# Edge layer of a four-layer image network: where the sum of VectorE's subtrahends is taken off

## The chip, the cores and the metric

The kernel runs on one core of one Trainium2 chip. The metric is the device time of one execution in microseconds (us); of several executions the median is given. Everything is in 32-bit floating point.

## The reference

The network takes four images of 56 x 56 positions with 128 channels and applies four layers: a windowed attention with a feed-forward part, an edge layer on the rows of the image, a spectral attention and a convolution over rows. The change touches the second layer alone. Its reference is, with one row of 56 nodes for each l:

```python
W1, W2 = (We[:, :f], We[:, f:])
proj_i = jnp.einsum('blnf,of->blno', x, W1)
proj_j = jnp.einsum('blnf,of->blno', x, W2)
edge = jax.nn.relu(proj_i[:, :, :, None, :] + proj_j[:, :, None, :, :] + be)
edge_sum = edge.sum(axis=3)
node_in = jnp.concatenate([x, edge_sum], axis=-1)
node = jax.nn.relu(jnp.einsum('blnc,oc->blno', node_in, Wn) + bn)
```

For each node n of a row, and each of the 56 nodes m of the same row, a ReLU of the sum of two projections is formed, and the 56 results are added. With a the first projection and c the negated second one (bias included), what is added over m is relu(a[n] - c[m]). A group normalisation stands ahead of the layer, and the layer's input is added to its output.

## The kernel before

The four images are taken one after the other, and `edge_layer` runs once for each. It keeps the 128 channels on the partitions, and goes through the image in seven blocks j of 8 rows, 448 nodes (`NB`). In each block it goes through 14 **turns** g, numbered 0 to 13. A turn makes one tile t of four values of m: 4 x 448 = 1792 elements on each partition. The string that follows says which engine makes it:

```python
EDGE_TURNS = "ddpddpdpddpddp"
```

- In the nine turns marked d, VectorE takes the maximum of a and c in one instruction (tile e_td, L967, four buffers). As max(a, c) = relu(a - c) + c, each such value is too large by c[m]. The sum of c over the 36 values of m that VectorE handles is called `rest`, one number for each row and channel (e_rest, L984, a reduce on VectorE, in turn 9).
- In the five turns marked p (2, 5, 7, 10 and 13), GpSimd forms a - c (tile e_tp, L969, three buffers), and ScalarE applies the ReLU in place (L971).

After each turn PE adds the tile to the accumulator e_acc (L974): 16 quadrants of 32 x 32 with an identity as weights, in 32 instructions, since each fp32 product is two. The 128 partitions of the tile are so spread that e_acc has four parts. When all 14 turns are added, ScalarE copies the accumulator to SBUF (e_sums, L986). There is one accumulator, so turn 0 of the next block waits for this copy.

The output of a block (`output`) is made in the next block, after its turn 2: PE multiplies the normalised input by Wn's first half (L940), `rest` by the negated second half (e_nWn, L941), and the four parts of e_sums by the second half (L944), all added into the bank e_po. Each product is again two instructions. In turn 7 of that next block, VectorE finishes the block (`finish`, L949): bias, ReLU, and the sum with the layer's input. After turn 5 of a block ScalarE evacuates the projections of the block that follows (`evacuate`, L932 to L935), and after the copy of the sums PE makes the projections of the block after that (`project`, L922 and L924).

PE, ScalarE and VectorE take the layer's instructions in the order in which the source writes them. GpSimd's order within the layer is chosen by a scheduler. Each engine works through its own queue in order, and a tile's buffer is free for its next use when PE has added it.

Of the kernel before, what the change touches and what calls it, by code (L numbers as in the profile page):

```python
# [13 lines left out]
ALU = mybir.AluOpType  # L14
AX = mybir.AxisListType
# [5 lines left out]
HH = 56  # L21
TOK = HH * HH
NB = 448
# [8 lines left out]
def bc(ap, axis, n):  # L32

    ap = ap.unsqueeze(axis)
    shape = list(ap.shape)
    shape[axis] = n
    return ap.to_broadcast(shape)


def blk(j):  # L40
    return slice(j * NB, (j + 1) * NB)
# [149 lines left out]
def apply_norm(k, out, xt, mr):  # L191
    k.nc.vector.tensor_scalar(out, xt, mr[:, 0:1], mr[:, 1:2], ALU.subtract, ALU.mult)
# [698 lines left out]
EDGE_TURNS = "ddpddpdpddpddp"  # L891


def edge_layer(k, w, x1, st):

    nc, tc = k.nc, k.tc  # L900
    xf = x1.rearrange("p l n -> p (l n)")
    nd = 4 * EDGE_TURNS.count("d")
    quarters = [slice(32 * q, 32 * q + 32) for q in range(4)]
    with ExitStack() as es:
        big = es.enter_context(tc.tile_pool(name="e_big", bufs=1))
        wk = es.enter_context(tc.tile_pool(name="e_wk", bufs=2))
        psum = es.enter_context(tc.tile_pool(name="e_ps", bufs=2, space=PSUM))

        def bank():
            return psum.tile([P, 512], F32, tag="mm", name="e_mm")  # L910

        mr = group_norm_factors(k, wk, bank, st)
        xg = big.tile([P, TOK], F32, name="e_xg")
        for j in range(NBLK):
            apply_norm(k, xg[:, blk(j)], xf[:, blk(j)], mr)
        ready = {}

        def project(j):
            if j >= NBLK:
                return  # L920
            pa = psum.tile([P, 512], F32, tag="pa", name="e_pa")
            nc.tensor.matmul(pa[:, :NB], w.W1, xg[:, blk(j)], start=True, stop=True)  # L922
            pc = psum.tile([P, 512], F32, tag="mm", name="e_pc")
            nc.tensor.matmul(pc[:, :NB], w.W2, xg[:, blk(j)], start=True, stop=True)  # L924
            ready[j] = pa, pc

        def evacuate(j):
            if j >= NBLK:
                return
            pa, pc = ready[j]  # L930
            c = wk.tile([P, 8, HH], F32, name="e_c")
            nc.scalar.activation(c.rearrange("p l m -> p (l m)"), pc[:, :NB], AF.Identity, bias=w.nbe, scale=-1.0)  # L932
            a = wk.tile([P, NB], F32, name="e_a")
            nc.scalar.copy(a, pa[:, :NB])  # L934
            nc.scalar.activation(xf[:, blk(j)], xf[:, blk(j)], AF.Identity, bias=w.bn)  # L935
            ready[j] = pa, a, c

        def output(j, rest, sums):
            po = psum.tile([P, 512], F32, tag="mm", name="e_po")
            nc.tensor.matmul(po[:, :NB], w.Wn[:, 0, :], xg[:, blk(j)], start=True, stop=False)  # L940
            nc.tensor.matmul(po[:, :NB].rearrange("p (l n) -> p l n", l=8), w.nWn, bc(rest, 2, HH),  # L941
                             start=False, stop=False)
            for r in range(4):
                nc.tensor.matmul(po[:, :NB], w.Wnq[:, r, :], sums[:, r, :], start=False, stop=(r == 3))  # L944
            return po

        def finish(j, po):

            nc.vector.scalar_tensor_tensor(xf[:, blk(j)], po[:, :NB], w.nbn, xf[:, blk(j)], ALU.max, ALU.add)  # L949

        with tc.manual_schedule(engines={mybir.EngineType.PE, mybir.EngineType.Activation, mybir.EngineType.DVE}):
            for j in range(2):
                project(j)
                evacuate(j)
            last = None
            for j in range(NBLK):
                pa, a, c = ready.pop(j)
                acc = psum.tile([P, 4, 512], F32, name="e_acc", bufs=1)
                rest = wk.tile([P, 8], F32, name="e_rest")
                at = {"d": 0, "p": nd}  # L960
                for g, e in enumerate(EDGE_TURNS):
                    t = wk.tile([P, 4, 8, HH], F32, tag="e_" + e, name="e_t" + e, bufs=4 if e == "d" else 3)
                    cm = bc(c[:, :, at[e]:at[e] + 4].rearrange("p l m -> p m l"), 3, HH)
                    at[e] += 4
                    if e == "d":
                        am = bc(pa[:, :NB].rearrange("p (l n) -> p l n", l=8), 1, 4)
                        nc.vector.tensor_tensor(t, am, cm, ALU.max)  # L967
                    else:
                        nc.gpsimd.tensor_sub(t, bc(a.rearrange("p (l n) -> p l n", l=8), 1, 4), cm)  # L969
                        tf = t.rearrange("p m l n -> p (m l n)")  # L970
                        nc.scalar.activation(tf, tf, AF.Relu)  # L971
                    for q in range(4):
                        for r, o in enumerate(quarters):
                            nc.tensor.matmul(acc[quarters[q], r, :NB], k.ident[o, o],  # L974
                                             t[o, q].rearrange("p l n -> p (l n)"),
                                             start=(g == 0), stop=(g == len(EDGE_TURNS) - 1))
                    if g == 2 and last:
                        po = output(*last)
                    if g == 5 and last:
                        evacuate(j + 1)  # L980
                    if g == 7 and last:
                        finish(last[0], po)
                    if g == 9:
                        nc.vector.tensor_reduce(rest, c[:, :, 0:nd], AX.X, ALU.add)  # L984
                sums = wk.tile([P, 4, NB], F32, name="e_sums")
                nc.scalar.copy(sums, acc[:, :, :NB])  # L986
                last = j, rest, sums
                project(j + 2)
            finish(last[0], output(*last))


def edge_weights(k, w, pool):

    for n, t in (("nbe", w.be), ("nbn", w.bn), ("nWn", w.Wn[:, 1, :])):
        r = pool.tile(list(t.shape), F32, name="e_" + n)
        k.nc.vector.tensor_scalar_mul(r, t, -1.0)
        setattr(w, n, r)
# [1325 lines left out]
def group_norm_factors(k, pool, bank, st):  # L2323

    nc = k.nc
    mv = pool.tile([P, 2], F32, tag="mv", name="gf_mv")
    nc.vector.bn_aggr(mv, st.rearrange("p a b -> p (a b)"))
    ps = bank()
    nc.tensor.matmul(ps[:, 0:1], k.g4, mv[:, 0:1], start=True, stop=True)
    mr = pool.tile([P, 2], F32, tag="mr", name="gf_mr")  # L2330
    nc.vector.tensor_copy(mr[:, 0:1], ps[:, 0:1])
    t = pool.tile([P, 1], F32, tag="gt", name="gf_t")
    nc.vector.tensor_sub(t, mv[:, 0:1], mr[:, 0:1])
    nc.vector.tensor_mul(t, t, t)
    nc.vector.tensor_add(t, t, mv[:, 1:2])
    ps = bank()
    nc.tensor.matmul(ps[:, 0:1], k.g4, t, start=True, stop=True)
    nc.scalar.activation(t, ps[:, 0:1], AF.Sqrt, bias=k.eps)
    nc.vector.reciprocal(mr[:, 1:2], t)
    return mr  # L2340
# [6 lines left out]
def build(k, packs, I, out):  # L2347
# [3 lines left out]
    with ExitStack() as es:  # L2351
# [12 lines left out]
        with tc.tile_pool(name="w01", bufs=1) as wp, tc.tile_pool(name="io", bufs=1) as io:  # L2364
# [30 lines left out]
            def first_layers(attention, x, to, loaded=False):  # L2395
                if not loaded:
                    nc.sync.dma_start(xw, x)
                xf = io.tile([P, TOK], F32, name="xf")
                attention(k, w0, xw, xf)
                st = io.tile([P, 9, 6], F32, name="x1_st")  # L2400
                mlp(k, w0, xf, xw, x1, st)
                edge_layer(k, w1, x1, st)
                nc.sync.dma_start(to, x1)
# [62 lines left out]
```

## Time and profile before

| what | value |
|---|---|
| median of 8 executions | 3926.8 us (3921.81 to 3933.76) |
| profiled execution, its own time | 3933.63 us |
| its span | 3931.8 us |
| mean granted PE clock, whole span | 0.954 |
| PE, VectorE, ScalarE, GpSimd busy, share of the span | 90%, 73%, 52%, 31% |
| one tile of VectorE (L967), GpSimd (L969), its ReLU (L971) | 2.017, 3.262, 1.697 us |
| reduce (L984), copy of the sums (L986), finish (L949) | 0.444, 1.652, 0.684 us |

The table is to be read with two things in mind. The shares of busy time are averages over all four layers; what holds the edge layer is seen only in its own stretches, of which the first goes from about 610 to 769 us. And the duration of an instruction is longer than the step to the next one on the same engine: seven tiles of VectorE in a row take 13.61 us, 1.94 each. In a line of the timeline, the brackets give how long the engine was idle ahead of the instruction, and whose work ended that idling; "issue" means that the profile shows nothing that it waited for. PEld is the loading of weights for a matmul, and its start shows when PE comes to a turn.

### The profile page before, as it was taken

The page shows a single profiled execution, that of the slowest core. Times are in us where ns is not written, and L with a number is a line of the kernel's source. Part 1 is how long each engine was busy: PE and PEld are TensorE (multiplying, and loading weights), DVE is VectorE, ACT ScalarE, POOL GpSimd, SP SyncE. Part 2 cuts the span into 40 slices and gives each one's busy share as a digit, 9 for nine tenths or more (in the row PEclk, how much of TensorE's full clock was granted, in tenths as well). Part 3 has the DMA queues.
Part 4 walks back from the last instruction along what each step waited for, and adds up shares of the span by engine and source line. Part 5 has one row for each costly group of instructions (what it writes and reads, how often), then busy time and mean ns, then how long its engine had stood idle before and what let it go on. Part 6 is the DMA issues. An engine that isn't in the chain of part 4 may idle for free. (4 is left out here: it accounts for less than half of the span.)

```text
span 3931.8 us, 79380 instructions
## 1 busy us (share of the span) xinstructions
PE 3551.7 (90%) x35416; PEld 1589.2 (40%) x35416; DVE 2883.9 (73%) x2667; ACT 2048.2 (52%) x2056; POOL 1200.9 (31%) x671
## 2 busy tenths in 40 slices
PE   6899988989998898999889999998977989999988
PEld 4322234552222455322245532223446433336554
DVE  6588877748887785888768668885875767775664
ACT  4577755457775454777645567773532002215332
POOL 0000006600000570000037200001860869984665
PEclk8999989999999999999999999998988999999988
DMA  2000000000000000000000000000022047842101
GB/s 94 1 1 1 1 1 19 19 1 1 1 1 1 18 3 17 1 1 1 1 17 3 18 1 1 1 1 0 3 77 94 2 91 164 175 96 83 58 9 50
DMA packets 73497, 111.12 MB, mean 28 GB/s; under 512 B 62141, under 2 KB 63933, under 8 KB 67901
## 3 DMA queue, kind: packets, MB, share of 16 engines
q1 hardware_dynamic: 14460, 93.13, 8.0%
q10 hardware_dynamic: 58688, 12.85, 2.0%
q8 instruction: 279, 4.57, 0.5%
q14 instruction: 70, 0.57, 0.0%
HBM read 79.46 MB, written 26.51 MB: 27 GB/s over the span
## 5 line engine op out<-in xcount | busy, mean ns | idle before, releaser
L641 ACT ACTIVATE f_ring<-f_s 128x1792 f32<-128x1792 f32 (+3 forms) x796 | 1097.8, 1429 | 316.6 <-PE f_s L639 314.4
L594 DVE TENSOR_TENSOR f_acc<-f_acc,f_ring 128x1792 f32<-128x1792 f32 x560 | 1134.0, 2025 | 80.8 <-ACT f_ring L641 27.3
L639 PE MATMUL f_s<-f_qT,f_kT 32*128 32x448 f32 x5376 | 741.0, 573 | 57.6 <-ACT f_ring L641 24.0
L883 POOL TENSOR_TENSOR x<-xf,xw 128x343 f32<-128x343 f32 (+2 forms) x36 | 29.9, 832 | 2134.5 <-issue 2062.2
L600 PE MATMUL f_po<-f_ring,f_va 128*32 128x448 f32 x5376 | 591.2, 547 | 0.0
L967 DVE TENSOR_TENSOR e_td<-e_pa,e_c 128x1792 f32<-128x1792 f32 x252 | 491.4, 2017 | 8.0 <-ACT e_a L934 8.0
L969 POOL TENSOR_TENSOR e_tp<-e_a,e_c 128x1792 f32<-128x1792 f32 x140 | 451.7, 3262 | 143.5 <-PE e_acc L974 104.6
L639 PEld LDWEIGHTS f_s<-f_qT,f_kT 32*128 32x128 f32 x5376 | 269.0, 184 | 538.2 <-ACT f_ring L641 368.2
L974 PE MATMUL e_acc<-e_td,t_shared 32*32 32x448 f32 x8064 | 322.1, 545 | 25.9 <-DVE e_td L967 15.4
L971 ACT ACTIVATE e_tp<-e_tp 128x1792 f32<-128x1792 f32 x140 | 235.2, 1697 | 187.2 <-POOL e_tp L969 187.2
L1568 DVE TENSOR_TENSOR u_ud<-u_px,u_d 112x1792 f32<-112x1792 f32 x144 | 240.2, 1708 | 95.1 <-PE u_po L1573 86.0
L600 PEld LDWEIGHTS f_po<-f_ring,f_va 128*32 128x32 f32 x5376 | 132.9, 109 | 399.6 <-issue 398.6
L974 PE MATMUL e_acc<-e_tp,t_shared 32*32 32x448 f32 x4480 | 220.5, 544 | 2.5 <-ACT e_tp L971 2.2
L1573 PE MATMUL u_po<-u_ud,AT 112*64 112x448 f32 x960 | 200.7, 548 | 23.7 <-DVE u_ud L1568 23.7
L1570 POOL TENSOR_TENSOR u_up<-xh,u_d 112x1792 f32<-112x1792 f32 x64 | 193.7, 3053 | 24.1 <-PE u_po L1573 12.4
L974 PEld LDWEIGHTS e_acc<-e_td,t_shared 32*32 32x32 f32 x8064 | 133.6, 103 | 150.3 <-DVE e_td L967 60.5
L594 DVE TENSOR_TENSOR f_acc<-f_ring 128x1792 f32<-128x1792 f32 x28 | 56.7, 2025 | 106.0 <-ACT f_ring L641 76.3
L1573 PE MATMUL u_po<-u_up,AT 112*64 112x448 f32 x576 | 125.1, 541 | 0.9 <-POOL u_up L1570 0.9
L1573 PEld LDWEIGHTS u_po<-u_ud,AT 112*64 112x64 f32 x960 | 64.9, 137 | 147.9 <-issue 86.7
L974 PEld LDWEIGHTS e_acc<-e_tp,t_shared 32*32 32x32 f32 x4480 | 94.4, 103 | 54.6 <-ACT e_tp L971 18.6
L856 ACT ACTIVATE m_hT<-m_ph,w_fb 128x392 f32<-128x392 f32 x128 | 72.7, 588 | 73.6 <-PE m_ph L855 68.2
L612 DVE RECIPROCAL f_den<-f_s 128x448 f32<-128x448 f32 x28 | 82.8, 2956 | 37.6 <-PE f_s L610 37.6
(460 smaller groups left out, 4755.6 us busy)
## 6 DMA issues: line engine op xcount, KB each, us to landing
u_d<-dd SPq DMA_DIRECT2D x48, 784.0 KB
xw<-in_x SPq DMA_DIRECT2D x4, 1568.0 KB
x2d<-x SPq DMA_DIRECT2D x4, 1568.0 KB
x_xs<-xad ACTq DMA_DIRECT2D x32, 196.0 KB
xm<-x_ev ACTq DMA_DIRECT2D x64, 98.0 KB
o_a<-xm SPq DMA_DIRECT2D x8, 784.0 KB
o_x<-x2d SPq DMA_DIRECT2D x4, 1568.0 KB
out<-o_o SPq DMA_DIRECT2D x12, 448.0 KB
```

Of the source, the lines that this page charges most:

```text
L594: nc.vector.tensor_add(acc, slots(j, 0) if c == 1 else acc, slots(j, c))
L600: nc.tensor.matmul(po[heads[h], :NB], va[o, c, heads[h]], p, start=(c == 0), stop=(c == 24))
L612: nc.vector.reciprocal(den, pd[:, 0, :NB])
L639: nc.tensor.matmul(ss[:, i, :NB], kT[heads[h], c * P:(c + 1) * P], qT[heads[h], blk(j)], start=True, stop=True)
L641: nc.scalar.activation(ring[:, slot:slot + m, :], ss[:, :m, :NB], AF.Exp, scale=scale)
L967: nc.vector.tensor_tensor(t, am, cm, ALU.max)
L969: nc.gpsimd.tensor_sub(t, bc(a.rearrange("p (l n) -> p l n", l=8), 1, 4), cm)
L971: nc.scalar.activation(tf, tf, AF.Relu)
L974: nc.tensor.matmul(acc[quarters[q], r, :NB], k.ident[o, o], t[o, q].rearrange("p l n -> p (l n)"), start=(g == 0), stop=(g == len(EDGE_TUR ...
L1568: nc.vector.tensor_mul(u, bc(px[:, :, :NB], 2, m), dm)
L1570: nc.gpsimd.tensor_mul(u, bc(x, 2, m), dm)
L1573: nc.tensor.matmul(po[64 * b2:64 * b2 + 64, :NB], st.AT[:, 8 * i + h0 + q, 2 * bp + b2, :], u[:, b2, q, :], start=(left == 16), stop=(left ...
```

## The change

`rest` is computed in turn 0 of its block, after VectorE's first tile, in place of turn 9. GpSimd's tile of turn 10 is not added to the accumulator in its turn but held. In turn 13, after its own tile has been written down, the source has GpSimd subtract `rest` from one of the four values of m in the held tile (448 elements on each partition); then PE adds the held tile and turn 13's tile, in this order. The product of `rest` with e_nWn goes from `output`, and the negated half of Wn from `edge_weights`.

```diff
-        def output(j, rest, sums):
+        def output(j, sums):
             po = psum.tile([P, 512], F32, tag="mm", name="e_po")
             nc.tensor.matmul(po[:, :NB], w.Wn[:, 0, :], xg[:, blk(j)], start=True, stop=False)
-            nc.tensor.matmul(po[:, :NB].rearrange("p (l n) -> p l n", l=8), w.nWn, bc(rest, 2, HH),
-                             start=False, stop=False)
             for r in range(4):
...
                         nc.scalar.activation(tf, tf, AF.Relu)
-                    for q in range(4):
-                        for r, o in enumerate(quarters):
-                            nc.tensor.matmul(acc[quarters[q], r, :NB], k.ident[o, o],
-                                             t[o, q].rearrange("p l n -> p (l n)"),
-                                             start=(g == 0), stop=(g == len(EDGE_TURNS) - 1))
+                    if g == 0:
+                        nc.vector.tensor_reduce(rest, c[:, :, 0:nd], AX.X, ALU.add)
+                    elif g == 10:
+                        held = t
+                        continue
+                    elif g == 13:
+                        nc.gpsimd.tensor_sub(held[:, 0], held[:, 0], bc(rest, 2, HH))
+                    for p in (t,) if g < 13 else (held, t):
+                        for q in range(4):
+                            for r, o in enumerate(quarters):
+                                nc.tensor.matmul(acc[quarters[q], r, :NB], k.ident[o, o],
+                                                 p[o, q].rearrange("p l n -> p (l n)"),
+                                                 start=(g == 0), stop=(g == 13 and p is t))
                     if g == 2 and last:
                         po = output(*last)
...
-                    if g == 9:
-                        nc.vector.tensor_reduce(rest, c[:, :, 0:nd], AX.X, ALU.add)
                 sums = wk.tile([P, 4, NB], F32, name="e_sums")
                 nc.scalar.copy(sums, acc[:, :, :NB])
-                last = j, rest, sums
+                last = j, sums
...
-    for n, t in (("nbe", w.be), ("nbn", w.bn), ("nWn", w.Wn[:, 1, :])):
+    for n, t in (("nbe", w.be), ("nbn", w.bn)):
```

## The prediction

> **What bounds the kernel now.** I read the granted clock and busy shares first, then the table by windows for the edge layer, then the timeline of a few blocks, engine by engine. The edge layer runs four times (about 148 us each, from 619.7 to 768.0 us in the first sample), and one steady block of 448 columns repeats every 20.53 us at full clock. The table by windows for one such block (length; busy time of PE, weight loads, VectorE, ScalarE, GpSimd):
>
> ```profile
> 660.28:680.81 20.53, 20.35 (x465) 10.74 (x465) 18.42 (x12) 11.34 (x9) 16.14 (x6) 1.00 0.01 2
> ```
>
> PE looks full with 20.35 of 20.53 us, and that is misleading; what sets the period is a loop over four engines. The timeline of the same block (start, duration, engine, line, operation, idle before it and who ended the idle):
>
> ```profile
> 660.28 1.65 ACT L986 COPY e_sums<-e_acc 128x1792 f32<-128x1792 f32 x1 [2.88 <-PE e_acc L974]
> 661.98 0.24 PEld L974 LDWEIGHTS e_acc<-e_td,t_shared 32*32 32x32 f32 x32 [0.77 <-ACT e_sums L986]
> 665.00 0.30 PEld L940 LDWEIGHTS e_po<-e_xg,t_edge 128*128 128x128 f32 x2 [0.73 <-issue]
> 665.48 0.19 PEld L941 LDWEIGHTS e_po<-e_rest,e_nWn 128*128 128x128 f32 x1 [0.19 <-issue]
> 665.86 0.19 PEld L941 LDWEIGHTS e_po<-e_rest,e_nWn 128*128 128x128 f32 x1 [0.19 <-issue]
> 666.24 0.19 PEld L944 LDWEIGHTS e_po<-e_sums,t_edge 128*128 128x128 f32 x1 [0.19 <-issue]
> ...
> 669.71 0.23 PEld L974 LDWEIGHTS e_acc<-e_td,t_shared 32*32 32x32 f32 x32 [0.65 <-issue]
> 669.82 0.68 DVE L949 SCALAR_TENSOR_TENSOR x<-e_po,e_nbn,x 128x448 f32<-128x448 f32 x1 [2.11 <-PE e_po L944]
> 670.42 3.95 DVE L967 TENSOR_TENSOR e_td<-e_pa,e_c 128x1792 f32<-128x1792 f32 x2
> 672.94 9.69 POOL L969 TENSOR_TENSOR e_tp<-e_a,e_c 128x1792 f32<-128x1792 f32 x3 [4.39 <-PE e_acc L974]
> 674.28 0.44 DVE L984 TENSOR_REDUCE e_rest<-e_c 128x8 f32<-128x288 f32 x1
> 674.64 7.81 DVE L967 TENSOR_TENSOR e_td<-e_pa,e_c 128x1792 f32<-128x1792 f32 x4
> 678.64 0.25 PEld L974 LDWEIGHTS e_acc<-e_td,t_shared 32*32 32x32 f32 x32 [0.94 <-DVE e_td L967]
> 679.42 0.55 PEld L974 LDWEIGHTS e_acc<-e_tp,t_shared 32*32 32x32 f32 x31 [0.27 <-issue]
> 680.81 1.65 ACT L986 COPY e_sums<-e_acc 128x1792 f32<-128x1792 f32 x1 [2.88 <-PE e_acc L974]
> ```
>
> Call S the start of the copy of the sums (660.28) and F the start of the finish (669.82). The loop is: copy (the one accumulator is free at S+1.70), PE turns 0, 1, 2 (to 665.00), twelve matmuls of the last block's output (665.00 to 669.71), finish on VectorE, which has stood idle 2.11 us for it, then VectorE's turns 8 and 9, the reduce, turns 11 and 12, then PE's turn 12 (which ended PE's last real wait, 0.94 us), turn 13, and the next S. 1.70+3.02+4.82 gives F = S+9.54; F to the next S is 10.99; together 20.53. GpSimd is not in the loop: it waits 4.39 us for a buffer of e_tp.
>
> In the first block of a layer there is no output, and GpSimd runs without a gap:
>
> ```profile
> 632.67 1.70 ACT L971 ACTIVATE e_tp<-e_tp 128x1792 f32<-128x1792 f32 x1 [1.52 <-POOL e_tp L969]
> 635.89 1.70 ACT L971 ACTIVATE e_tp<-e_tp 128x1792 f32<-128x1792 f32 x1 [1.52 <-POOL e_tp L969]
> 638.35 0.55 PEld L974 LDWEIGHTS e_acc<-e_tp,t_shared 32*32 32x32 f32 x31 [0.27 <-issue]
> 639.75 1.65 ACT L986 COPY e_sums<-e_acc 128x1792 f32<-128x1792 f32 x1 [2.16 <-PE e_acc L974]
> ```
>
> These are the ReLUs of GpSimd's fourth and fifth tile (turns 10 and 13); the fifth is ready at 637.59, just before PE takes it.
>
> [...] 20.35 us busy, yet PE waited 0.94 us for VectorE and 0.77 us for the copy. [...] here 0.73 and 0.65 us of "issue" stand at the two changes around the output. The change keeps both, so they are not saved. [...] the trace's full tile has 1792 elements in 3.262 us, which scales to 0.82 us.
>
> **The change part by part.**
>
> 1. *The product with e_nWn goes.* It is two instructions per block (56 in all for 28 blocks). Their loads step by 0.38 us (665.48, 665.86, 666.24), so 0.76 us of PE, and VectorE's 2.11 us of idling at F shows that this lies on the loop: F = S+8.78. In the last block of each layer it saves nothing: there the sums' matmuls wait for the copy (load at 764.65 after 0.76 us, copy started at 762.95), and the removed product ran inside that wait. So it counts in six loops of a layer, not seven blocks.
>
> 2. *The reduce moves from turn 9 to turn 0.* Behind turn 9 it takes 0.36 us of VectorE's way from F to turn 12 (674.28 to 674.64). At turn 0 it lies ahead of F, in the 2.11 us of idling; if that cover were gone it would cost its 0.36 us again. Worth 0.36 us in each loop. In the first block it is ahead of turn 12 in either place: nothing.
>
> 3. *Turn 10's tile is accumulated after turn 12.* PE's count of turns is the same, but a turn leaves the stretch where PE is ahead of VectorE (it would wait longer for turn 11 and 12) and joins the tail behind turn 12, where nothing hides it. Two turns there take 2.13 us (658.11 to the last matmul's end at 660.24 in the block before). Three turns after an idle stretch took 3.08 us (669.71 to 672.79, turns 3 to 5). The third costs 0.95 us; the low bound is the 0.77 us from start to start of turns 12 and 13, the high bound 1.36 us, a turn's matmuls with nothing overlapping. I take 0.95.
>
> 4. *GpSimd gets one difference of 448 elements per block.* In the compiled order of the changed kernel it stands right behind turn 10's tile and ahead of turn 13's, not where the source has it. It needs ScalarE's ReLU of turn 10, so GpSimd stands still for 1.7 us and then works for about 0.90 us ([...]a row of 343 elements, L883, takes 0.91). Behind it wait turn 13's tile and, through that, ScalarE's ReLU and PE's turn 13.
>    - First block: the fourth tile ends at 632.65, its ReLU at 634.37, the difference at about 635.3, the fifth tile at 638.55, its ReLU at 640.27; PE takes it at 640.30, and as PE is then idle its turn ends in 1.05 us: S = 641.40 in place of 639.75. **+1.65 us** once per layer.
>    - Steady block: the held buffer comes free only some 0.7 us before S, so GpSimd's turn 5 of the next block runs from S-0.7 to S+2.5, turn 7 to S+5.8, turn 10 to S+9.0, ReLU to S+10.7, the difference to S+11.7. Turn 13 waits in any case for turn 5's buffer, until F+3.12 = S+11.9 (672.94 against 669.82). So the stop is hidden by the 4.39 us of idling; even after that its ReLU ends at F+8.1 and PE wants it at F+10.0. Cover 1.9 us beyond the 0.2; past that each us is paid in every block.
>
> 5. *The rest.* The setup's 128x128 negation on VectorE goes, once: nothing seen, at most 0.2 us. No DMA is added, removed or passed, SP's queue is unchanged, and VectorE's new wait of the reduce on GpSimd's difference of two blocks before is long satisfied.
>
> **Sum.** A loop: -0.76 - 0.36 + 0.95 = -0.17 us. A layer: 1.65 - 6 x 0.165 = +0.66 us. Four layers: **+2.6 us**, less up to 0.2. With 0.77 for the extra turn: 4 x (1.65 - 6 x 0.345) = -1.7 us; with 1.36: +12.5 us. So the gain of 27 us that the removed rows alone would give (24 loops x 1.12 us) is given back twice: 22.8 us on PE's tail and 6.6 us in four first blocks. The profiled execution took 3933.63 us (span 3931.8), 0.17% above the median of 3926.8; the sum is made on its durations and should carry over: about 3929 us. 0.2% is 7.9 us, about what a measurement of this kernel tells from no change, so I forecast no difference.
>
> **Rivals.**
> - *Slower: GpSimd's stop gets into the loop.* The place is turn 13's tile. It decides against the kernel from a difference of about 2.3 us on (each 0.1 us costs 0.4 us in first blocks alone), and past 3.0 us in every block. If subtracting eight repeated values took as long as a whole tile (3.26 us): first blocks 1.65 + 2.36, loops late by 0.25: 4 x (4.01 - 1.0 + 1.5) = +18 us, 3945. For it: everything behind it is in one in-order queue. [...] The extra turn past 1.18 us would cross 0.2% too. Together 0.20.
> - *Faster: the extra turn is no extra.* If PE's own throughput, not VectorE's turn 12, ended the block, 14 turns would cost the same in any order: 4 x (1.65 - 6 x 1.12) = -20 us, 3907; it crosses 0.2% where the third turn costs under 0.52 us. For it: PE busy in 99% of the block, turns 6 to 10 spaced 0.95 us. Against: the 0.94 us of waiting for turn 12. 0.17.
> - *The removed product is not on the path* (part of the same end, slower): then a loop gains 0.36 and pays 0.95, in all +21 us; VectorE's idling at F speaks plainly against it, and its chance is in the 0.20.
>
> **How the numbers follow.** No difference has 0.63; its own range is 3924 to 3934, from the two prices of the extra turn and 0.1 to 0.2 us of doubt on each first block. To hold 8 in 10 the range reaches part of both rivals, 3914 to 3942; the ends of -20 and +18 stay outside.
>
> **What would show it.** In the profile after: no rows of e_rest into e_po; S to F 8.8 us for 9.5; VectorE idle about 1.7 us at F; the gap from turn 12's load to S about 3.1 us in place of 2.2; the period 20.3 to 20.4; the first block's S 1.6 to 1.7 us later from its first VectorE tile; GpSimd's small difference at 0.8 to 1.0 us after a wait of 1.7 for ScalarE. I am wrong if the period is under 20.0 or over 20.7, or if PE's turn 13 waits for ScalarE in steady blocks.

## The result and the profile after

**The changed kernel is slower by 0.35%.** Its median is 3942.82 us (19 executions, 3934.98 to 3946.78) beside 3928.5 us for the kernel before (51 executions), a ratio of 1.0035 with a 95% interval of 1.0029 to 1.0041. The forecast of no difference is wrong, and 3942.82 lies 0.8 us outside the range. The profiled execution took 3940.39 us (span 3938.4), 6.8 us more than that of before.

The timeline of one steady block after the change (start, duration, engine, line, operation, idle before it and who ended the idle) answers to the block shown of before:

```profile
658.37 1.65 ACT L991 COPY e_sums<-e_acc 128x1792 f32<-128x1792 f32 x1 [2.81 <-PE e_acc L981]
660.07 0.24 PEld L981 LDWEIGHTS e_acc<-e_td,t_shared 32*32 32x32 f32 x32 [0.76 <-ACT e_sums L991]
663.09 0.30 PEld L941 LDWEIGHTS e_po<-e_xg,t_edge 128*128 128x128 f32 x2 [0.73 <-issue]
663.57 0.19 PEld L943 LDWEIGHTS e_po<-e_sums,t_edge 128*128 128x128 f32 x1 [0.19 <-issue]
...
667.15 0.69 DVE L948 SCALAR_TENSOR_TENSOR x<-e_po,e_nbn,x 128x448 f32<-128x448 f32 x1 [1.95 <-PE e_po L943]
669.02 0.94 POOL L977 TENSOR_TENSOR e_tp<-e_tp,e_rest 128x448 f32<-128x448 f32 x1 [1.81 <-ACT e_tp L970]
670.22 6.48 POOL L968 TENSOR_TENSOR e_tp<-e_a,e_c 128x1792 f32<-128x1792 f32 x2 [0.26 <-PE e_acc L981]
675.62 0.24 PEld L981 LDWEIGHTS e_acc<-e_td,t_shared 32*32 32x32 f32 x32 [1.54 <-DVE e_td L966]
676.40 0.56 PEld L981 LDWEIGHTS e_acc<-e_tp,t_shared 32*32 32x32 f32 x32 [0.27 <-issue]
677.15 0.75 PEld L981 LDWEIGHTS e_acc<-e_tp,t_shared 32*32 32x32 f32 x31 [0.19 <-issue]
677.41 0.45 DVE L972 TENSOR_REDUCE e_rest<-e_c 128x8 f32<-128x288 f32 x1
678.74 1.65 ACT L991 COPY e_sums<-e_acc 128x1792 f32<-128x1792 f32 x1 [3.53 <-PE e_acc L981]
```

The loads of e_sums (L943) follow those of e_xg (L941) at once: the product with e_nWn is gone. S to F is 667.15 - 658.37 = 8.78 us. GpSimd's difference takes 0.94 us after 1.81 us of waiting for ScalarE, and the tile behind it still has to wait 0.26 us for PE: the stop is hidden here. In the tail there are now three turns behind PE's wait (675.62, 676.40, 677.15), and the copy starts 3.12 us after the first of them. The period is 678.74 - 658.37 = 20.37 us, against 20.53 before. The table by windows has for the block that follows (length; busy time of PE, weight loads, VectorE, ScalarE, GpSimd; granted clock; DMA share; GB/s):

```profile
678.74:699.12 20.38, 19.60 (x463) 9.97 (x464) 18.43 (x12) 11.33 (x10) 17.11 (x7) 1.00 0.01 3
```

PE is 0.75 us less busy than in the block shown of before (19.60 for 20.35), GpSimd 0.97 more (17.11 for 16.14), VectorE the same (18.43 for 18.42), and the clock is full.

In the first block of the layer:

```profile
629.07 1.70 ACT L970 ACTIVATE e_tp<-e_tp 128x1792 f32<-128x1792 f32 x1 [1.52 <-POOL e_tp L968]
630.85 0.94 POOL L977 TENSOR_TENSOR e_tp<-e_tp,e_rest 128x448 f32<-128x448 f32 x1 [1.81 <-ACT e_tp L970]
635.03 1.70 ACT L970 ACTIVATE e_tp<-e_tp 128x1792 f32<-128x1792 f32 x1 [4.26 <-POOL e_tp L968]
...
638.00 1.65 ACT L991 COPY e_sums<-e_acc 128x1792 f32<-128x1792 f32 x1 [1.27 <-PE e_acc L981]
```

The gap between the last two ReLUs is 4.26 us where it was 1.52. From the first VectorE tile (616.09) to S it is 21.91 us; before it was 639.75 - 619.69 = 20.06. So the first block loses 1.85 us, and a layer, from its first VectorE tile to the start of its last finish, takes 149.2 us in place of 148.3.

Four layers, then, cost 3.7 us more (the third is 151.3 us, 150.3 before, in the profiled executions). The larger part of the difference lies in the **last stage**: from the first product of the row convolution's o_y (L1806, after L1811) to the end. No line of the diff is in it. In the table by windows, first before, then after:

```profile
3548.00:3931.80 383.80, 341.07 (x2200) 221.68 (x2200) 223.76 (x389) 142.79 (x198) 221.52 (x132) 0.89 0.11 43
```
```profile
3547.40:3938.40 391.00, 346.92 (x2200) 227.59 (x2200) 223.62 (x389) 142.96 (x198) 221.54 (x132) 0.87 0.11 43
```

The same number of instructions on every engine, the same busy time on VectorE, ScalarE and GpSimd, and 7.2 us more. What differs is PE: 5.9 us more busy, at a mean granted clock of 0.87 for 0.89. The other stages of the two profiles differ by -3.6 us (start to the first edge layer), +0.9 in sum (between the edge layers) and -1.5 (behind the fourth, up to the last stage). With 3.7 and 7.2 that is the 6.6 us of the two spans. The first of these is no effect of the change: the kernel before alone took 619.7 us for that stretch in one profile and 614.7 in another, and 561.3 and 555.8 between its first two edge layers.

### The profile page after: what moved, and what is told of

Same layout as the page of the kernel before. It is cut to its first block, busy times and chain, and to the rows that moved or that the text cites. A ratio compares the mean times of both kernels' runs of the same rounds, so it can differ in the third digit from the quotient of the medians.

```text
span 3938.4 us, 79347 instructions
## 1 busy us (share of the span) xinstructions
PE 3535.9 (90%) x35360; PEld 1574.9 (40%) x35360; DVE 2883.7 (73%) x2666; ACT 2050.1 (52%) x2056; POOL 1227.0 (31%) x699
## 5 line engine op out<-in xcount | busy, mean ns | idle before, releaser
L981 PE MATMUL e_acc<-e_td,t_shared 32*32 32x448 f32 x8064 | 301.6, 545 | 47.0 <-DVE e_td L966 38.6
L981 PE MATMUL e_acc<-e_tp,t_shared 32*32 32x448 f32 x4480 | 200.3, 544 | 3.5 <-ACT e_tp L970 3.5
L981 PEld LDWEIGHTS e_acc<-e_td,t_shared 32*32 32x32 f32 x8064 | 124.9, 103 | 178.6 <-DVE e_td L966 95.6
```

The lines of the kernel that those rows point to most:

```text
L981: nc.tensor.matmul(acc[quarters[q], r, :NB], k.ident[o, o], p[o, q].rearrange("p l n -> p (l n)"), start=(g == 0), stop=(g == 13 and p is t))
```

## Where PE's clock falls

The mean of 0.87 is not a steady slower clock: the trace's clock records know only 1.0 and 0.5. Every half-clock stretch in them but the last, which runs to the end of the records, is a whole multiple of 3.413 us long (38 stretches in each of the two profiles, of 1 to 10 times 3.413 us before and 1 to 11 times after), and within one execution they all end at one phase of a grid of 3.413 us (to 0.01 us in these two). Counted in windows of that length, the last stage has 26 at half clock before, and 30 after. They fall on different work. PE's timeline, before and then after, at the same two places of the stage:

```profile
3598.95 4.96 PE L1859 MATMUL o_d<-o_z,t_images 56*112 56x448 f32 x16 [1.55 <-ACT o_z L1843]
...
3613.42 3.34 PE L1837 MATMUL o_d<-t_images,o_t 128*128 128x64 f32 x28
```
```profile
3598.32 3.27 PE L1864 MATMUL o_d<-o_z,t_images 56*112 56x448 f32 x16 [1.54 <-ACT o_z L1848]
...
3612.40 6.24 PE L1842 MATMUL o_d<-t_images,o_t 128*128 128x64 f32 x28
```

The first 16 matmuls are fast in the kernel after (3.27 us) and slow before (4.96), the later 28 the other way round (6.24 and 3.34). The clock records have a half-clock stretch from 3599.48 to 3602.89 us before, and one from 3609.52 to 3623.17 after. What sets the clock to one half, no run here tests. The 26 windows of this stage alone are 89 us at half clock (26 times 3.413), up to 44 us of lost time or 1.1% of the span (an estimate, for PE as the limit), and two to ten more of them are what decides a question of 0.35%. It is no mere chance from run to run: two executions of the kernel before took 383.8 us each for the stage, though the grid stood at 1.58 us in one and 2.22 us in the other when they began.

**The theory** that I tested is: the edge layer costs what the prediction's parts say, and any change of a few tenths of a us ahead of the last stage moves the instant at which that stage starts within a window (called its **place**, 0 to 3.413 us, measured at its first o_y product), and with it how many windows fall to half clock. The runs bear out the second half of this, and not the first: a shift far ahead is forgotten (see the delays). **The rival**: the difference belongs to the edge change itself, through a part of the work that the first profile doesn't show (an order changed further on, buffers, GpSimd's stop), and would follow the edge layer's instructions.

## The experiments

Each was compared with the kernel before on its own chip. "Edge layers" is the sum of the four layers' changes; an edit that only delays has its delay in "own delay" instead. The last stage and its place are those of one profiled execution. The first two rows are of the two given kernels.

| kernel | median, us | ratio to before (95%) | edge layers | own delay | last stage | place | median less before |
|---|---|---|---|---|---|---|---|
| before | 3928.5 | | | | 383.8 | 3.15 | |
| after | 3942.82 | 1.0035 (1.0029 to 1.0041) | +3.7 | | 391.0 | 2.77 | +14.3 |
| before_again | one run: 3922.74 | | | | 383.8 | 3.21 | |
| after_again | one run: 3947.43 | | +4.3 | | 394.4 | 2.78 | |
| in_place2 | 3919.55 | 0.9982 (0.9973 to 0.9990) | -17.4 | | 391.8 | 2.78 | -9.0 |
| on_vector2 | 3925.61 | 0.9992 (0.9981 to 1.0002) | -13.4 | | 398.0 | 2.87 | -3.0 |
| reduce_first | 3920.58 | 0.9983 (0.9975 to 0.9991) | -8.6 | | 387.0 | 3.37 | -7.2 |
| delay_each2 | 3940.1 | 1.0027 (1.0019 to 1.0035) | | 3.0 | 394.4 | 2.83 | +11.5 |
| delay_first | 3939.15 | 1.0019 (1.0006 to 1.0031) | | 0.7 | 394.4 | 2.81 | +9.7 |
| delay_third | 3939.41 | 1.0031 (1.0019 to 1.0042) | | 0.7 | 398.0 | 2.89 | +9.9 |
| delay_last2 | 3937.06 | 1.0023 (1.0013 to 1.0033) | | 0.8 | 386.8 | 0.09 | +8.5 |
| delay_last4 | 3934.99 | 1.0020 (1.0011 to 1.0030) | | 1.7 | 391.0 | 2.74 | +6.5 |
| delay_last7 | 3938.52 | 1.0025 (1.0017 to 1.0032) | | 3.0 | 394.4 | 2.76 | +10.1 |
| after_nudge | 3939.97 | 1.0026 (1.0014 to 1.0038) | +4.3 | | 386.9 | 0.12 | +12.2 |
| before_nudge | 3938.24 | 1.0032 (1.0019 to 1.0045) | | | 392.1 | 0.91 | +10.5 |
| in_place_nudge | 3915.18 | 0.9966 (0.9954 to 0.9978) | -17.7 | | 386.8 | 0.19 | -12.6 |

### Parts of the change: in_place2, on_vector2, reduce_first

**in_place2** keeps the whole change but the held tile: `rest` is taken off GpSimd's turn 10 in turn 10, and PE adds every tile in its own turn.

```diff
                     elif g == 10:
-                        held = t
-                        continue
-                    elif g == 13:
-                        nc.gpsimd.tensor_sub(held[:, 0], held[:, 0], bc(rest, 2, HH))
-                    for p in (t,) if g < 13 else (held, t):
+                        nc.gpsimd.tensor_sub(t[:, 0], t[:, 0], bc(rest, 2, HH))
```

> As the changed kernel, but the tile of turn 10 is added in its own turn, right after GpSimd's subtraction, so no turn is moved behind turn 12. Tail theory (the moved turn costs about 0.95 us a loop, the stop of GpSimd about 1.85 us in each first block): the period falls from 20.37 to about 19.4 us, an edge layer takes 148.3 + 1.85 - 6 x 1.12 = 143.5 us in place of 148.3 before, so the four layers lie 19 us under before. Rival (the moved turn costs nothing, GpSimd's stop is what holds the steady block): the period stays at 20.4 and a layer at 149. Whatever lies outside the edge layers adds between 0 and +10 us to the total if it belongs to the change itself, and may have either sign if it is the granted clock of later stages: total between -19 and -9 us against before.

ScalarE's copies of the sums in its timeline:

```profile
653.08 1.65 ACT L987 COPY e_sums<-e_acc 128x1792 f32<-128x1792 f32 x1 [1.85 <-PE e_acc L977]
...
672.50 1.65 ACT L987 COPY e_sums<-e_acc 128x1792 f32<-128x1792 f32 x1 [2.43 <-PE e_acc L977]
```

The period is 19.42 us, which is 20.53 - 0.76 - 0.36 to 0.01 us, and a layer takes 143.5 us. That is 5.7 us under the changed kernel's 149.2, and 5.7 is six loops of 0.95: the third turn in the tail, and nothing else. The edge layers gain 17.4 us, less than the 19 expected, because the third one gains only 3.1 us where the others gain 4.7 to 4.8; the last stage gives 8.0 of them back (391.8 for 383.8), and the measured gain is 9.0.

**reduce_first** is the kernel before with the reduce alone moved:

```diff
-                    if g == 9:
+                    if g == 0:
                         nc.vector.tensor_reduce(rest, c[:, :, 0:nd], AX.X, ALU.add)
```

> The kernel before with the reduce moved from turn 9 to turn 0 and nothing else; the product with the negated weights stays. Edge layer by my sum: period 20.53 - 0.36 = 20.17 us, layer 148.3 - 6 x 0.36 = 146.2 us, four layers 8.6 us under before. Rival (VectorE's idle time does not hide the reduce at turn 0): period 20.5, layer 148.3. Total: the 8.6 us less whatever the outputs stage loses by another time of arrival, so between -9 and +2 us.

A layer takes 146.2 us in place of 148.3, so four gain 8.6, which is 24 loops of 0.36 us. The part is worth what the prediction said. The last stage took 387.0, and the median is 7.2 us better.

**on_vector2** takes `rest` off one of VectorE's own tiles, in turn 3, instead of one of GpSimd's:

```diff
-                    elif g == 10:
-                        held = t
-                        continue
-                    elif g == 13:
-                        nc.gpsimd.tensor_sub(held[:, 0], held[:, 0], bc(rest, 2, HH))
+                    elif g == 3:
+                        nc.vector.tensor_sub(t[:, 0], t[:, 0], bc(rest, 2, HH))
```

> As the changed kernel, but VectorE subtracts the sum, from one value of its own tile of turn 3, where it would otherwise wait for the output; GpSimd has no part in it and all turns are added in their own place. Tail theory: period 20.53 - 0.75 - 0.36 = 19.4 us, since VectorE's 0.5 us for 448 elements fits into its idle time ahead of the finish (1.95 us in the changed kernel, about 0.9 us left here before it); first block later by 0.5 us only; layer 148.3 + 0.5 - 6.7 = 142.1 us; four layers 25 us under before. Rival (VectorE is then full and becomes the bound): period 19.6 to 19.9, layer 144 to 145.5, four layers 11 to 17 us under before. Outside the edge layers as in the kernel without the moved turn.

The trace's answer for that line gives shortest, median and longest duration in ns, and below it stand two of the 28 in VectorE's timeline:

```profile
L974 DVE TENSOR_TENSOR e_td<-e_td,e_rest x28: 716/1076/2311, 614.0 to 2857.1; 128x448 f32<-128x448 f32 x28
```
```profile
652.79 1.06 DVE L974 TENSOR_TENSOR e_td<-e_td,e_rest 128x448 f32<-128x448 f32 x1
...
672.22 1.91 DVE L974 TENSOR_TENSOR e_td<-e_td,e_rest 128x448 f32<-128x448 f32 x1
```

The subtraction takes 1.43 us in the mean, and its length changes from block to block for the same 448 elements: 1.06 us in the first of the two, 1.91 in the second. (The finish, of as many elements, takes 0.67 or 0.68 us in all 28 blocks of this trace.) What lengthens it, no run here tests. So 0.5 us, which is a quarter of a maximum's 2.017, was the wrong price, and of the two expectations the rival came true: VectorE is full. Blocks of 19.43 and 20.28 us take turns (19.86 in the mean), and VectorE no longer idles ahead of the finish; in this block it is busy for 20.25 us of 20.28:

```profile
668.26:688.54 20.28, 19.59 (x463) 9.78 (x464) 20.25 (x14) 11.34 (x10) 17.37 (x6) 1.00 0.01 3
```

A layer takes 145.0 us (142.1 and 144 to 145.5 were the two forecasts). It gains 3.3 us, and the last stage gives 14.2 back: the ratio's interval holds 1.

### The edge change left out: delays

If the loss of the last stage does not need the edge change, then the kernel before must be able to show it too when it is only delayed. The delay multiplies the block of 448 columns that the last finish of a layer has just written by one, on VectorE:

```diff
             finish(last[0], output(*last))
+            for _ in range(2):
+                nc.vector.tensor_scalar_mul(xf[:, blk(6)], xf[:, blk(6)], 1.0)
```

Two of them take 0.82 us, as VectorE's timeline shows for delay_last2:

```profile
2897.78 0.82 DVE L994 TENSOR_SCALAR x<-x 128x448 f32<-128x448 f32 x2
```

Behind the first three layers VectorE's instructions of the next attention stand around and between the two multiplications. In delay_first VectorE comes to the next attention's w_qd (L224) 5.27 us after the layer's last finish began, in the kernel before 4.54 us, so the delay is 0.73 us there.

**delay_each2** has it in every layer; **delay_last2**, **delay_last4** and **delay_last7** in the fourth alone, with 2, 4 and 7 multiplications.

> The kernel before with two multiplications by 1.0 (448 elements, VectorE) behind the last block of each edge layer, about 0.9 us on the path each time, which is the lengthening of an edge layer that the changed kernel shows (149.2 for 148.3 us), without its change. Content theory (the 10 us outside the edge layers come from the changed program itself: other addresses, other instructions): +3.6 us in all, nothing in the outputs stage. Clock theory (the outputs stage gets another granted clock because the program reaches it at another time): the outputs stage moves by several us from 383.8, either way, and the total by another amount than 3.6, +14 if the time of arrival is all that counts.

> The kernel before with the same two multiplications behind the last edge layer only, 0.9 us once. Content theory: +0.9 us, within the noise of before. Clock theory: the later stages shift by 0.9 us only, and their granted clock and time change by several us either way, the outputs stage away from 383.8 us.

> The kernel before with four multiplications by 1.0 behind the last edge layer, about twice the delay of the kernel with two (which gave 8.5 us on the median for 0.9 us of delay). Cost theory (what is added is simply paid, with some factor): more than with two, +10 us or above. Arrival theory: no such order; the total may well be smaller than with two, between -2 and +12 us, with the later stages' half-clock stretches in other places.

> The same with seven multiplications, about 3 us of delay, near the 3.41 us of which every half-clock stretch in the profiles is a whole multiple. Cost theory: more than with four. Arrival theory: the program comes back to nearly the same place against that grid, so the later stages run as in before and the total is about +3 us, less than with two.

All four are slower than the sum of their delays: 8.5 us for 0.82, 6.5 for about 1.7, 10.1 for about 3.0 (about +3 in all was expected) and 11.5 for about 3.0. No edge instruction is changed, and the last stage is 3.0 to 10.6 us longer. That speaks against the rival. But the place did not move by the delay: delay_last7 arrived at 2.76, where delay_last4 and the changed kernel do. The delay itself is gone before: the stage ahead of the last one, the attention's application, starts at 1.39 on the grid in the kernel before, and at 1.36, 1.34 and 1.41 behind delays of 0.82, 1.7 and 3.0 us. And each delay is also two or more instructions more, so these runs do not separate time from content.

**delay_first** and **delay_third** put the two multiplications into the first or the third layer alone.

> The kernel before with two multiplications by 1.0 (0.82 us) behind the first edge layer only, some 2800 us ahead of the outputs stage. Resynchronising theory (between two layers the program passes stretches at half clock that end on the 3.41 us grid, and forgets a small shift): the outputs stage is reached at 3.2 us after a grid point again and takes 383.8 us, the total moves by no more than a few us. Rival (a shift is carried through to the end): arrival at another place, stage at 387 to 394 us and total up by 6 to 11 us as with the same delay behind the last layer.

> Two multiplications (0.82 us) behind the third edge layer only, one attention layer and one edge layer ahead of the place where the same delay cost 8.5 us. Resynchronising theory: the half-clock stretches of one attention are enough, stage 383.8 us, total within a few us of before; or not enough, then stage 387 to 394 us. Rival: as with the delay behind the last layer.

In delay_first the start of the third edge layer, the start of the fourth's last finish and VectorE's first multiplication in the attention's application stand at 0.22, 2.74 and 1.40 on the grid; in before_again at 0.22, 2.75 and 1.45. So between the first layer and there the kernel does fall back into step with itself, a delay of 0.82 us notwithstanding. Yet the last stage was not 383.8 us again, as expected, but 394.4: the stage in between, the attention's application, took 353.0 us in place of 353.3, and the place at the end of it was 2.81. Comparing the two traces instruction by instruction on VectorE, the whole 0.3 us arises at one multiplication of that stage, 229.8 us after PE's first product there. VectorE's timeline of before_again, then of delay_first:

```profile
3415.72 3.96 DVE L1568 TENSOR_TENSOR u_ud<-u_px,u_d 112x1792 f32<-112x1792 f32 x2 [2.32 <-PE u_po L1573]
```
```profile
3423.34 3.95 DVE L1574 TENSOR_TENSOR u_ud<-u_px,u_d 112x1792 f32<-112x1792 f32 x2 [1.97 <-PE u_po L1579]
```

The wait is put down to PE in both, 2.32 us in one and 1.97 in the other, although the matmuls ahead of it began at the same moment (227.65 and 227.67 us after PE's first product). From this multiplication to the first o_y product it is 121.5 us in both.

This wait sorts all sixteen profiles. It is 2.32 us in the kernel before (both times), before_nudge and reduce_first, and 1.97 us in the twelve others. The first four are those with exactly 2214 VectorE instructions ahead of it; the changed kernel has 2213, because the negation in `edge_weights` is gone, on_vector2 2241, and the kernels with a delay 2216 to 2222. The line of reduce_first, then that of the changed kernel:

```profile
3411.59 4.95 DVE L1568 TENSOR_TENSOR u_ud<-u_px,u_d 112x1792 f32<-112x1792 f32 x3 [2.32 <-PE u_po L1573]
```
```profile
3425.95 4.95 DVE L1573 TENSOR_TENSOR u_ud<-u_px,u_d 112x1792 f32<-112x1792 f32 x3 [1.97 <-PE u_po L1578]
```

Fourteen of the sixteen profiles begin this stage at 1.33 to 1.58 on the grid, whatever their edge layers and delays were. The other two (the first of the changed kernel, at 3.09, and on_vector2, at 3.14) are back in step within 36 us. So the 0.35 us that part the place of the kernel before (3.15 and 3.21) from that of most others (2.74 to 2.89) do not come from the length of the edge layer. They go with the number of VectorE's instructions in the program, of which the change takes one out. What the 0.35 us are, the trace doesn't name, and no run changed that number alone, so the cause of this wait stays open.

### The same kernels, run once more, and nudged

**before_again** and **after_again** are the two kernels unchanged, for one more profile each.

> The kernel before, unchanged, for a second profile of its stages. Arrival theory (the granted clock of the outputs stage follows from when the program reaches it, and this is nearly the same in every execution of one program): outputs stage within about 3 us of 383.8 and the edge layers at 148.3 again. Rival (each execution draws its clock at random): the outputs stage lies anywhere between 384 and 398 us, the span of the profiles so far.

> The changed kernel, unchanged, for a second profile of its stages. Arrival theory: outputs stage within about 3 us of 391.0, edge layers 149.2 again. Rival: anywhere between 384 and 398 us.

The table by windows of the last stage, before_again and then after_again:

```profile
3537.20:3921.00 383.80, 340.99 (x2200) 221.70 (x2200) 223.63 (x389) 142.83 (x198) 221.57 (x132) 0.89 0.11 43
```
```profile
3551.10:3945.50 394.40, 350.08 (x2200) 229.38 (x2200) 224.81 (x389) 142.65 (x197) 221.51 (x132) 0.86 0.11 42
```

The kernel before repeats to 0.1 us. The changed kernel arrives at the same place (2.78, 2.77) and is 3.4 us longer than the first time, which misses the expectation (within 3 us of 391.0). The place of the first product decides much, not all.

A **nudge** is one more small VectorE instruction (0.0 times 336 elements of the last product, added to as many of the last image; 0.51 us) at the very end of the attention's application, just ahead of the last stage:

```diff
                 nc.vector.tensor_add(im, im, pc)
+                if turn == len(turns) - 1:
+                    nc.vector.scalar_tensor_tensor(im[:, :6], pc[:, :6], 0.0, im[:, :6], ALU.mult, ALU.add)
```

**after_nudge**, **before_nudge** and **in_place_nudge** are the kernels after, before and in_place2 with it. One edit is to help two of them and to hurt the third, if the last stage's time follows its place.

> The changed kernel with one more VectorE instruction (336 elements, adds zero times the last product to the last images) right ahead of the outputs stage, about 0.4 to 0.5 us on its path. The profiles so far: the stage takes 383.8 us where its first product starts 3.15 to 3.21 us after a grid point of 3.41 us (the kernel before, twice), and 391.0 to 394.4 where it starts at 2.74 to 2.83. Arrival theory: the added work moves the changed kernel from 2.77 to about 3.2, the stage takes 383.8 to 387 us, and the total falls by 4 to 10 us against the changed kernel's (to +1.0 to +2.5 in thousandths of before, from +3.5). Rival (the stage is slower for what the changed kernel is): the total rises by 0.5 us.

> The kernel before with the same instruction. Arrival theory: it leaves its place at 3.2 for about 0.2 us after a grid point, where the kernel with 0.9 us of delay stood at 0.09 and took 386.8 us: stage 386 to 391 us, total up by 3 to 7 us, which is the other sign than in the other two kernels. Rival: +0.5 us.

> The kernel that adds turn 10 in its own place, with the same instruction ahead of the outputs stage. Its first product stood at 2.78 us after a grid point and its stage took 391.8 us. Arrival theory: stage 383.8 to 387 us, total 5 to 8 us lower than its 3919.6, so about 3912 to 3915, faster than every kernel so far. Rival: 3920.

The last stage by windows: after_nudge, before_nudge, in_place_nudge.

```profile
3552.50:3939.40 386.90, 344.11 (x2200) 223.84 (x2200) 223.61 (x389) 142.89 (x198) 221.50 (x132) 0.88 0.11 42
```
```profile
3536.70:3928.80 392.10, 349.45 (x2200) 230.94 (x2200) 223.76 (x389) 142.81 (x198) 221.80 (x132) 0.86 0.11 42
```
```profile
3529.60:3916.40 386.80, 344.03 (x2200) 223.83 (x2200) 223.62 (x389) 142.89 (x198) 221.59 (x132) 0.88 0.11 42
```

The stage goes from 391.0 or 394.4 down to 386.9 in the changed kernel, from 391.8 down to 386.8 in in_place2's, and from 383.8 up to 392.1 in the kernel before: one instruction, with both signs. Half-clock windows: 28, 28 and 33. The place moved by more than the 0.4 to 0.5 us expected, by 0.8 in the first two and 1.1 in the kernel before, so that they arrived at 0.12 and 0.19, and not near 3.2, and at 0.91, and not near 0.2. Over the medians before_nudge loses 10.5 us (3 to 7 were expected). in_place_nudge gains 3.6 us on in_place2 (5 to 8 were expected), 0.9966 (0.9954 to 0.9978) to 0.9982 (0.9973 to 0.9990), though these two intervals overlap; it is the fastest of all kernels here. after_nudge is not shown to be faster than the changed kernel: 1.0026 (1.0014 to 1.0038) overlaps 1.0035 (1.0029 to 1.0041), and 12.2 us of loss are more than the 4.3 + 3.1 of its profile.

**What the runs show together.** In order of the place the last stage took: 0.09 to 0.19: 386.8 to 386.9 (three kernels); 0.91: 392.1; 2.74 to 2.89: 391.0 to 398.0 (nine profiles); 3.15 and 3.21: 383.8; 3.37: 387.0. The times go with the half-clock windows: 26 of them at 383.8 us, 28 at 386.8 to 387.0, 30 at 391.0, 32 at 394.4, 33 at 391.8 and 392.1, 36 at 398.0. Kernels with quite different edge layers (in_place2, after, delay_last7) fall into the same band at the same place, and the kernel before, moved by the nudge, leaves its time. That the last stage's time changes when its place is moved is shown by the nudges. Might it be the added instruction and not the place? The number of instructions alone does not decide: delay_first, delay_third and delay_last2 have the same one, and took 394.4, 398.0 and 386.8 us at the places 2.81, 2.89 and 0.09. That the edge layer's instructions are not needed for the loss is shown by the delays, and so much of the rival is excluded; that the content of the program has a hand in the place, by the number of VectorE's instructions, is not. The place of the kernel before has the shortest last stage of all that occurred, and each of the other kernels lost it; that is luck of the kernel before, and not a merit of its edge layer.

The sum of edge layers, own delay and last stage agrees with the difference of the medians to 5 us or so: it gives -9.4 for -9.0 in in_place2, -5.4 for -7.2 in reduce_first, 10.9 to 14.9 for 14.3 in the changed kernel, but 14.9 for 9.9 in delay_third and 3.8 for 8.5 in delay_last2. One profile is one execution, and those of one kernel scatter (delay_first's from 3921.55 to 3951.16), so a finer account isn't to be had from these. A good part of that scatter lies ahead: the start to the first edge layer takes 607.7 to 619.7 us in the sixteen profiles.

## Why the prediction was wrong, point by point

- **The edge layer was predicted right.** S to F 8.78 us (8.8 forecast), the period 20.37 (20.3 to 20.4), turn 12's load to S 3.12 (about 3.1), GpSimd's difference 0.94 us (0.8 to 1.0, my estimate) after 1.81 (1.7), no row of e_rest into e_po. Its three prices of a loop are shown: -0.36 by reduce_first, -0.76 by in_place2's period (1.11 together with the -0.36), and +0.95 by the 5.7 us between in_place2's layer and that of the changed kernel.
- **VectorE's idling at F was read wrongly.** I forecast about 1.7 us by taking the reduce off the 2.11. It is 1.95: VectorE's busy time in a block is 18.43 us as before, so its only idle time is the period less that, 20.38 - 18.43 in the table by windows. The moved reduce is only moved.
- **The first block was sized 0.2 us too low**, 1.85 for 1.65. Up to the ReLU of turn 10 it is the same (14.68 us from the first VectorE tile in both kernels). GpSimd's step from there to turn 13's ReLU is 0.06 us longer than forecast, and PE's last turn, from its load (636.78) to S, takes 1.22 us for 1.10. That makes the layer's +0.66 into +0.9, and four layers' +2.6 into +3.7.
- **GpSimd's stop stayed out of the loop**, as forecast, with 0.26 us of waiting left behind it (0.2 forecast). The rivals' mechanisms did not occur: PE's turn 13 waits for nobody in the steady blocks, GpSimd's difference is far from a whole tile's 3.26 us, the removed product was on the path, and the extra turn is an extra.
- **The step that failed** is the sentence that the sum "is made on its durations and should carry over". It took every other stage as fixed. The edge layers' +3.7 us alone would have been 0.09%, about 3930.5 us for the 3929 forecast; the last stage added 7.2 us in one profile and 10.6 in the other, because it began at another place of the clock's grid and had 30 and 32 windows at half clock for 26. So "slower" came true by a route that stood among no rival. The same held on the other side: of the 17.4 us that in_place2 gains, 9.0 arrive. How the change comes to move the place is known only in part: 0.35 us of it arise at one wait of VectorE's in the stage ahead, and go with the one VectorE instruction that the change takes out of the set-up, for which the forecast had put "at most 0.2" us.
- **A warning stood in the trace of before.** In the last stage the granted clock was 0.89 while the edge layer had 1.00. And the clock records there show 26 windows at half clock, each worth up to 1.7 us where PE is the limit (an estimate, half of 3.413; the profiles have 1.1 to 1.8 us for each window more). A range that took in some eight windows either way, 14 us, would have held the result; without the experiments I would not have known that the number must be so large.

## What to carry to other kernels

Before a sum over one stage is carried to the whole, look at the granted clock of every stage behind it: where it is below 1 in the middle of steady work, as in the last stage here (0.89), the time of that stage may depend on when it begins (383.8 to 398.0 us here), and a change of 0.2 to 0.4% can be that alone. Judge such a change by the stage it touches, from the trace, and try the same kernel with a nudge just ahead of the stage in question; a gain or loss in that stage that one idle instruction undoes isn't a merit or fault of the change. A delay far ahead is a poorer test: this program had forgotten it. And a tile that is held back pays for its turn where it is added: ahead of the wait it was free, behind it it cost 0.95 us in each of 24 loops; in its own place the same change makes the kernel faster.

## What the runs showed of the hardware that I had not expected

- The last stage has the same 2200 matmuls in all kernels, and took from 383.8 to 398.0 us, with 26 to 36 windows of 3.413 us at half clock. One VectorE instruction just ahead of it changed it by -4 to -8 or by +8 us.
- The long program falls back into step with the grid: of two executions of the kernel before, begun at grid phases of 1.58 and 2.22 us, the last stage began at 3.15 and 3.21, and 14 of 16 profiles of quite different kernels began the stage ahead of it at 1.33 to 1.58. How this comes about was not tried.
- One wait of VectorE's in that stage was 2.32 us in the four profiles with 2214 VectorE instructions ahead of it, and 1.97 us in the twelve with another number. With the point above, this makes the effect repeat with a kernel and look like a property of its change.
- VectorE's subtraction of 448 elements in on_vector2 took from 0.72 to 2.31 us (28 times, 1.43 in the mean), where the finish, of as many elements, took 0.67 or 0.68 us each time.
